# A graph network with experts on one Trainium2 core: other places for the experts' buffers, the second z weights loaded earlier, source rows made by TensorE, marks in bfloat16, and bounds and first attention weights within z

## The chip, the cores and the metric

The kernel runs on one core of one Trainium2 chip, in one launch. Its time is the device time in microseconds (us), the median over several runs. One of its executions is also recorded by the hardware profiler; all durations of single instructions come from that record. The engines are called as the profile calls them: PE is TensorE (matrix products and transposes), PEld its loading of weights, DVE is VectorE, ACT is ScalarE, POOL is GpSimd, SP is SyncE. SP and POOL also issue DMA transfers, each in the order of its own queue, and an engine's q (PEq, POOLq) is its sequencer, which runs branches and issues.

## The reference

There are 1250 nodes with 1024 features and 20000 edges `src -> dst`. Four parts follow each other, each on a layer norm of x and each added to x:

1. Graph attention with 4 heads of 256 columns. `z = norm(x) W`, `el = z . a_l`, `er = z . a_r` for each head; for every edge `e = leaky_relu(el[src] + er[dst], 0.2)`; over the edges into each node a softmax of e; the node's new value is the sum of `alpha * z[src]`.
2. A feed-forward part: small block matrices ("rails"), a GELU, and a large projection `h @ w_cproj.T` with 16384 inner columns.
3. A graph convolution: `h = norm(x) W + b`, and a sum of `h[col]` over edges and self loops, scaled by the square roots of the degrees.
4. A shared GEGLU expert, plus, for each row, the one of 8 experts with the largest logit: `gelu(x w1) * (x w2) @ w3`.

## The kernel before

All sizes are fixed: 1250 rows are 10 tiles (`T`) of 125 rows (`R`). Nearly everything is float32. The work is written in program order, and the framework orders each engine's instructions from it, with waits where buffers or data demand them; pools give buffers their places in SBUF, on the left or on the right side. A buffer in a place that something else held waits for the last use of what lay there.

**Counts and z(0), to 155 us.** For every tile the edges become counts of edges between nodes: one-hot rows `os` and `od` (kept in a pool with `HOT` buffers each) and PE products `pc` (L335). The counts go to DRAM (`cnt_d`), are turned into `CT` (int16: for each source tile all destinations), and `mark` (L296) writes `nm`, which is -1e30 where two nodes have no edge and 0 where they have one, to `nm_d`. In the same loop a tile of x (`xt`, `load_x`) is normalized and turned into `xT`, and `z_tile(0, t)` (L215) multiplies it with the weights of heads 0 and 1: 16 matmuls L218, a copy by ACT (L219) and four sums by DVE (L223), which give el and er. The weights come by `z_weights(g)` (L207): 8 transfers of 256 KB into `W` and two 250 KB broadcasts of a_l and a_r into `aw`, all issued by POOL. `W` has one buffer. `Z[0]` lies in `BZ`, a place that later stages use again, `Z[1]` in a buffer of its own.

**Branch L375.** Edges outside the expected windows are counted again under a condition, which does not hold for these inputs. Every engine runs the branch (L376).

**z(1), 165 to 236 us.** The same products for heads 2 and 3. Beside them DVE computes, for heads 0 and 1, the maxima over sources: `maxima(0)` (L394) adds a tile's marks `nm2` (loaded by SP from `nm_d`, 547 KB each) to `els`, the el of all sources in one row that all 125 partitions hold, and takes the maximum (L401): 20 of them. `els` comes by `el_rows` (L198): one transposition, a row written to DRAM, and a broadcast load, both issued by POOL. `degrees(t)` (L315) sums CT's rows, for the graph convolution's degrees. Then `bounds(0)` (L405) turns the maxima into two rows per head: for head 0 by 20 transposes of a column spread over all columns (L425), for head 1 through DRAM.

**Attention, 245 to 460 us.** `attend(h, b, between)` (L499) does one head and one half of the destinations: for each of ten source tiles DVE makes `u` (L504), ACT its exponential (L505), DVE the weights `w` (L508: times the count), and PE five products (L510) that add up in `po`; DVE then scales and adds to `X` (L520). Between the steps of the second and third call DVE runs `maxima(1)`, for heads 2 and 3, whose `els` is made by `el_rows(1)`. `X` is loaded by POOL (L448).

**Projection, to 2300 us.** The feed-forward part as a plan of fast matrix products in blocks (L675 in `product`), then the graph convolution (L1051 and around, to 2510 us), whose PE products read `xT`'s place last at about 2499 us.

**Shared expert and experts, 2510 us to the end.** `hidden` (L1118 and on; products `pab` at L1125) for the shared expert reads its weights `w12s` from `BZ`. The normalized rows lie in `xn_d` in DRAM, and POOL scatters the token list `tok`. For each expert, `weights12` and `weights3` load 2 MB and 1 MB (issued by SP, L987 to L992), an indirect transfer by POOL gathers up to 224 rows in two parts into `xg` (L1215), PE turns them (L1221), `hidden` and a product L1231 follow, and the result goes to `ys_d`. At the end the rows are gathered from there and added.

Of the kernel before, what the change touches and what calls it, by code (L numbers as in the profile page):

```python
# [30 lines left out]
GS, GD, HI, LO = 50, 25, 5, 250  # L31
HOT = 27
NEG = -1.0e30
# [69 lines left out]
def gnn_ffn_kernel(ctx, tc, x, src, dst, gat_w, a_l, a_r, maker, up, cproj,  # L103
# [15 lines left out]
    cnt_t = cnt_d.rearrange("g m l -> (g m l)").rearrange("(c p t j) -> t p c j", c=T, p=R, t=T)  # L119
    nm_d = dram.tile([GS, R, LO], F32, name="nm_d")  # L120
    nm_t = nm_d.rearrange("g m l -> (g m l)").rearrange("(t r n) -> t r n", t=T, r=R)
# [54 lines left out]
    Z = (BZ[:R].rearrange("p (t h f) -> p t h f", t=T, h=2), zp.tile([R, T, 2, F + 1], F32, name="Z"))  # L176
    for z in Z:
        nc.gpsimd.memset(z[:, :, :, F:F + 1], 1.0)
    deg = zp.tile([R, T, T], F32, name="deg")
    el, er, mx, el2, el8 = (zp.tile([R, H, T], F32, name=n) for n in ("el", "er", "mx", "el2", "el8"))  # L180
    xT = xTp.tile([P, KD, NP], F32, name="xT")
    elp = gat.enter_context(tc.tile_pool(name="elp", bufs=1, side="right"))

    def to_row(pool, psp, cols, k, n):
# [9 lines left out]
    def spread(dst_t, row):  # L194

        nc.gpsimd.dma_start(dst_t, row.rearrange("k r -> (k r)").partition_broadcast(R))

    def el_rows(g, pool, psp):  # L198
        els = elp.tile([R, 2, N], F32, name="els")
        spread(els.rearrange("p a n -> p (a n)"),  # L200
               to_row(pool, psp, el[:, 2 * g:2 * g + 2, :].rearrange("p h t -> p (h t)"), 2 * T, f"el{g}"))
        return els

    with tc.tile_pool(name="gw", bufs=1) as gwp, tc.tile_pool(name="gps", bufs=3, space=PSUM) as psp:
        W, aw = {}, {}

        def z_weights(g):  # L207
            W[g] = gwp.tile([P, KD, 2, F], F32, name="W")
            for k in range(KD):
                nc.gpsimd.dma_start(W[g][:, k], gat_w[2 * g:2 * g + 2, k * P:(k + 1) * P, :].rearrange("h p f -> p h f"))  # L210
            aw[g] = gwp.tile([R, 2, 2, F], F32, name="aw")
            for i, a in enumerate((a_l, a_r)):
                nc.gpsimd.dma_start(aw[g][:, i], a[2 * g:2 * g + 2, :].partition_broadcast(R))

# [11 lines left out]
        with tc.tile_pool(name="cc", bufs=1) as ccp, tc.tile_pool(name="cw", bufs=2) as cwp:  # L226
# [69 lines left out]
            def mark(d):  # L296
                nm = cwp.tile([R, HI, LO], F32, name="nm", bufs=1)
                nc.vector.tensor_scalar(nm, cns[d], 0.0, NEG, op0=ALU.is_equal, op1=ALU.mult)
                dma(nc.sync, nm_d[d * HI:d * HI + HI].rearrange("g m l -> m g l"), nm)

            def turn_counts(d):
                cn = cns[d]
                CTv = CT.rearrange("p (h a) n -> p a h n", a=2)
                for blocks in ([(g, 0) for g in range(4)], [(g, 1) for g in range(4)], [(4, 0), (4, 1)]):
# [7 lines left out]
                    else:  # L312
                        nc.scalar.copy(CTv[:, :, :, d0:d0 + GD], pt[:, :2].rearrange("p a (q h) -> p a h q", h=HI))

            def degrees(d):  # L315
                nc.vector.tensor_reduce(deg[:, d, :], CT[:, :, d * R:(d + 1) * R], AX.X, ALU.add)

            with tc.tile_pool(name="hot", bufs=1) as hotp, tc.tile_pool(name="gl", bufs=2) as lnp:
# [20 lines left out]
                def load_x(t):  # L339
                    xt[t] = lnp.tile([R, D], F32, name="xt", bufs=3)  # L340
                    dma(nc.sync, xt[t], x_t[t])

                for t in range(3):
                    load_x(t)
                z_weights(0)
                hots(0)
                count(0)
# [12 lines left out]
                for t in range(T):  # L360
# [9 lines left out]
                    if t + 3 < T:  # L370
                        load_x(t + 3)
                z_weights(1)
            els0 = el_rows(0, cwp, psp)

# [19 lines left out]
        def maxima(g, mxp, els):  # L394

            for d in range(T):
                nm = mxp.tile([R, N], F32, name="nm2", bufs=3 - g)
                dma(nc.sync, nm, nm_t[d])
                for h in (2 * g, 2 * g + 1):
                    sc = mxp.tile([R, N], F32, name="sc2")  # L400
                    nc.vector.tensor_tensor_reduce(sc, nm, els[:, h - 2 * g, :], scale=1.0, scalar=-3.0e38,  # L401
                                                   op0=ALU.add, op1=ALU.max, accum_out=mx[:, h, d:d + 1])
                    yield

        def bounds(g, pool, psp, rowp):  # L405
# [10 lines left out]
            for h in range(2):  # L416
                rows[2 * g + h] = rowp.tile([R, 2, N], F32, name="rr", bufs=2)
                if 2 * g + h == 0:

                    for i in range(2):  # L420
                        for t0 in range(0, T, 4):
                            n = min(4, T - t0)
                            pb = psp.tile([P, 4, R], F32, name="pt")
                            for t in range(n):
                                nc.tensor.transpose(pb[:R, t, :], bd[:, h, i, t0 + t:t0 + t + 1].to_broadcast([R, R]),  # L425
                                                    ident[:R, :R])
                            copy = nc.vector.tensor_copy if t0 == 4 else nc.scalar.copy
                            copy(rows[0][:, i, t0 * R:(t0 + n) * R], pb[:R, :n, :].rearrange("p a b -> p (a b)"))
                    continue
                spread(rows[2 * g + h].rearrange("p a n -> p (a n)"),  # L430
                       to_row(pool, psp, bd[:, h].rearrange("p a t -> p (a t)"), 2 * T, f"bd{2 * g + h}"))

        rows = {}
        rowst = ExitStack()
        rowp = rowst.enter_context(tc.tile_pool(name="rowp", bufs=1, side="right"))
        with tc.tile_pool(name="mx0", bufs=1) as mxp:
            search = maxima(0, mxp, els0)
            for t in range(T):
                for _ in range(3):
                    next(search, None)  # L440
                z_tile(1, t)
                degrees(t)
            bounds(0, mxp, psp, rowp)

# [50 lines left out]

    with tc.tile_pool(name="att", bufs=3) as atp, tc.tile_pool(name="aps", bufs=6, space=PSUM) as aps, \
            tc.tile_pool(name="tps0", bufs=2, space=PSUM) as tps:

        def attend(h, b, between=iter(())):  # L499
            po = [aps.tile([R, F + 1], F32, name="po") for _ in range(HT)]  # L500
            r1, r2 = (rows[h][:, i, b * HN:(b + 1) * HN] for i in range(2))
            for s in range(T):
                u = atp.tile([R, HN], F32, name="u")
                nc.vector.scalar_tensor_tensor(u, r1, el8[:, h, s:s + 1], r2, op0=ALU.add, op1=ALU.max)  # L504
                nc.scalar.activation(u, u, AF.Exp, bias=el2[:, h, s:s + 1])  # L505
                w = atp.tile([R, HN], F32, name="w")

                nc.vector.scalar_tensor_tensor(w, u, 2.0, CT[:, s, b * HN:(b + 1) * HN], op0=ALU.min, op1=ALU.mult)  # L508
                for i in range(HT):
# [13 lines left out]
        with tc.tile_pool(name="mx1", bufs=1) as mxp:  # L523
# [7 lines left out]

            nc.vector.tensor_reduce(dis, deg.rearrange("p d s -> p s d"), AX.X, ALU.add)
            nc.vector.tensor_scalar(dis, dis, 1.0, None, op0=ALU.add)
            nc.scalar.activation(dis, dis, AF.Sqrt)
# [576 lines left out]
    with back_end:  # L1111
# [3 lines left out]
        with tc.tile_pool(name="ab", bufs=2, space=PSUM) as abp, tc.tile_pool(name="tps", bufs=2, space=PSUM) as tps, \  # L1115
# [88 lines left out]

            with tc.tile_pool(name="w12", bufs=2) as w12p, tc.tile_pool(name="w3p", bufs=2) as w3p, \
                    tc.tile_pool(name="xg", bufs=3) as xgp, tc.tile_pool(name="xgT", bufs=2) as xgTp, \
                    tc.tile_pool(name="hp", bufs=2) as hp, tc.tile_pool(name="yp", bufs=3, side="right") as yp:
# [126 lines left out]
```

## Time and profile before

| | us |
|---|---|
| median of 3 runs | 2812.83 |
| lowest, highest | 2807.91, 2813.6 |
| the profiled execution, its own time | 2814.6 |
| its span (first to last record) | 2812.9 |
| PE busy | 2724.5 |
| DVE busy | 1604.8 |
| ACT busy | 887.3 |
| POOL busy | 781.1 |
| the 320 products of z (L218), 512 columns each | 141.5 |
| attention products of heads 0 and 1 (L510), first group of 400 | 96.7 |

The profile's page gives busy time by engine, the busy share in 40 slices of the span, the DMA queues, the chain of work that ended last, and the groups of instructions that cost most. Its trace answers closer questions: the list of waits (who waited for whom, for how long in total, how often, and the longest), the timeline of a stretch (start, length, engine, line, operation, `out<-in`, count, and in brackets the idle time before and what ended it), windows (busy time of each engine in a stretch, with the granted clock of TensorE, the share of the DMA engines in use, and GB/s), and all instructions of one line. Line numbers are those of the kernel before, unless a text says after.

### The profile page before, as it was taken

The numbers are of one execution on the slowest core, as the hardware profiler recorded it, in microseconds if no ns is written. First come the engines' busy times: TensorE is split into PE (matmuls) and PEld (weight loads), VectorE is DVE, ScalarE is ACT, GpSimd is POOL, SyncE is SP. The second block draws the span as 40 slices with busy tenths as digits, with TensorE's granted clock in tenths as the row PEclk, the third lists the DMA queues.
The fourth block names the chain that finished last, engine by engine and source line by source line (L and its number), as shares of the span: only waits on it lengthen the run. The fifth ranks groups of instructions, "written<-read, shape, count | busy, mean of one in ns | idle before, by whom it ended". The sixth has DMA issues, their size and how long they took to land. (4 is left out here: it accounts for less than half of the span.)

```text
span 2812.9 us, 31800 instructions
## 1 busy us (share of the span) xinstructions
PE 2724.5 (97%) x11009; PEld 1868.6 (66%) x11009; DVE 1604.8 (57%) x2704; ACT 887.3 (32%) x1545; POOL 781.1 (28%) x1118
## 2 busy tenths in 40 slices
PE   8989899999999999999999999999999999998997
PEld 5646677666766766667667667666666754765774
DVE  8766977755556566555556466555546764520124
ACT  2313235444343343343443443433432011210000
POOL 2011000234434434344344344343432110111001
PEclk9999999999999999999999999999999999999999
DMA  6464423579999999999999999999997540623665
GB/s 167 122 172 118 120 59 132 186 176 169 220 179 206 207 181 225 183 164 203 181 168 199 173 178 194 166 196 181 146 229 220 166 75 0 122 61 108 229 213 166
DMA packets 268759, 461.13 MB, mean 164 GB/s; under 512 B 49252, under 2 KB 145810, under 8 KB 267959
## 3 DMA queue, kind: packets, MB, share of 16 engines
q0 software_dynamic: 129296, 279.93, 57.7%
q1 hardware_dynamic: 139288, 179.00, 21.0%
q8 instruction: 94, 1.54, 0.2%
q14 instruction: 81, 0.66, 0.1%
HBM read 182.72 MB, written 276.09 MB: 163 GB/s over the span
## 5 line engine op out<-in xcount | busy, mean ns | idle before, releaser
L688 POOL DMA_DIRECT2D acc_d<-low x686 | 594.7, 867 | 906.4 <-ACT low L684 885.0
L684 ACT COPY low<-po 128x626 f32<-128x626 f32 x735 | 501.0, 682 | 951.1 <-PE po L675 895.2
L675 PE MATMUL po<-X,arena 128*128 128x313 f32 x2208 | 619.4, 427 | 0.5 <-DVE X L668 0.4
L675 PEld LDWEIGHTS po<-X,arena 128*128 128x128 f32 x2208 | 415.2, 189 | 176.2 <-ACT low L684 16.0
L675 PE MATMUL po<-low,arena 128*128 128x313 f32 x1520 | 429.4, 428 | 0.0
L675 PEld LDWEIGHTS po<-low,arena 128*128 128x128 f32 x1520 | 285.6, 189 | 121.1 <-ACT low L684 11.6
L675 PE MATMUL po<-X,first_w 128*128 128x313 f32 x776 | 222.1, 428 | 0.0
L675 PE MATMUL po<-X,BZ 128*128 128x313 f32 x720 | 206.8, 430 | 0.0
L675 PEld LDWEIGHTS po<-X,first_w 128*128 128x128 f32 x776 | 145.6, 189 | 62.7 <-ACT low L684 7.6
L675 PE MATMUL po<-low,first_w 128*128 128x313 f32 x624 | 178.7, 427 | 2.6 <-DVE low L668 1.6
L675 PEld LDWEIGHTS po<-X,BZ 128*128 128x128 f32 x720 | 136.2, 191 | 58.5 <-ACT low L684 5.8
L675 PEld LDWEIGHTS po<-low,first_w 128*128 128x128 f32 x624 | 117.4, 189 | 52.3 <-ACT low L684 4.4
L218 PE MATMUL pz<-W,xT 128*125 128x512 f32 x320 | 141.5, 600 | 7.8 <-PEq L376 7.8
L668 DVE TENSOR_TENSOR X<-X 128x626 f32<-128x626 f32 x125 | 101.0, 812 | 68.6 <-PE po L675 59.5
L675 PE MATMUL po<-low,BZ 128*128 128x313 f32 x480 | 137.8, 428 | 0.0
L668 DVE TENSOR_TENSOR arena<-arena 128x512 f32<-128x512 f32 x126 | 86.4, 688 | 63.9 <-PE po L675 63.3
L668 DVE TENSOR_TENSOR X<-X,low 128x626 f32<-128x626 f32 x105 | 84.7, 810 | 56.4 <-PE po L675 46.0
L675 PEld LDWEIGHTS po<-low,BZ 128*128 128x128 f32 x480 | 90.0, 189 | 38.5 <-ACT low L684 3.7
L510 PE MATMUL po<-BZ,w 125*125 125x257 f32 x400 | 96.7, 402 | 18.6 <-DVE w L508 17.4
L668 DVE TENSOR_TENSOR X<-low,X 128x626 f32<-128x626 f32 x101 | 82.6, 823 | 54.9 <-PE po L675 49.0
L218 PEld LDWEIGHTS pz<-W,xT 128*125 128x125 f32 x320 | 60.1, 191 | 80.7 <-issue 79.8
L660 ACT ACTIVATE X<-pz 128x626 f32<-128x626 f32 (+8 forms) x220 | 101.6, 524 | 17.9 <-PE pz L488 17.9
(308 smaller groups left out, 3384.8 us busy)
## 6 DMA issues: line engine op xcount, KB each, us to landing
acc_d<-low POOLq DMA_DIRECT2D x735, 313.0 KB, 6.2
arena<-in_cproj SPq DMA_DIRECT2D x148, 256.0 KB
w<-in_w SPq DMA_DIRECT2D x16, 1024.0 KB
BZ<-in_cproj SPq DMA_DIRECT2D x56, 256.0 KB
first_w<-in_cproj SPq DMA_DIRECT2D x52, 256.0 KB
nm<-nm_d SPq DMA_DIRECT2D x20, 546.9 KB
w3t<-in_w SPq DMA_DIRECT2D x8, 1024.0 KB
low<-acc_d SPq DMA_DIRECT2D x19, 313.0 KB
```

The source lines that it names most:

```text
L218: nc.tensor.matmul(pz, xT[:, k, t * R:(t + 1) * R], W[g][:, k], start=(k == 0), stop=(k == KD - 1))
L510: nc.tensor.matmul(po[i], w[:, i * R:(i + 1) * R], Z[h // 2][:, s, h % 2, :], start=(s == 0), stop=(s == T - 1))
L660: nc.scalar.activation(view(key)[:, :, n0 - n * NQ:n1 - n * NQ], pz[:, 2 * i:2 * i + 2, a + n0 - c0:a + n1 - c0], AF.Gelu)
L668: tt(view(k), *a, op=ALU.add if sign == "+" else ALU.subtract)
L675: nc.tensor.matmul(po[:, o, :NQ], view(x)[:, q, o * P:(o + 1) * P], view(y)[:, q, :], start=(i == q == 0), stop=(i + 1 == len(pairs) and q ...
L684: nc.scalar.copy(part, po[:, :, :NQ])
L688: sent[:] = [nc.gpsimd.dma_start(out=acc_d[p - 1, i - 1], in_=part, accum_op=ALU.add).ins]
```

## The change

- **Experts' places apart.** The pool of the experts' first weights (`w12`) moves to the right side, into xT's old place; the pool of gathered rows (`xg`) is opened first on the left, in a place that BZ does not cover.
- **Second z weights early.** `W` gets two buffers, and the second weights are asked for within the z(0) loop, at the third tile. The instructions as built show them on POOL right behind the first weights and the memsets of the limits, ahead of the zero fills of `tok_d` and `ys_d`.
- **Attention vectors on SP.** `aw` is loaded in a function of its own, `head_weights`, by SP and not by POOL.
- **Source row by PE.** For heads 0 and 1 `els` is made by `rows_by_array`: 20 transposes of a column spread over 125 columns, and six copies by ACT and DVE, in place of the way through DRAM. `bounds(0)` uses the same function for head 0, as before.
- **Marks in bfloat16.** `nm_d`, `nm` and `nm2` are bfloat16.
- **Places before the branch.** `nm` and `xt` lie in `Z[1]`, which nobody needs until z(1); the ones in `Z[1]`'s last column are set after the branch. `HOT` is 32 in place of 27.
- **Degrees on ACT.** Each tile's sum is a copy by ACT with an accumulated output; the last sum over tiles goes.
- **Bounds and first weights within z.** `bounds(0)` stands before the eighth tile of z(1), and the first three weights of attention before the tenth; the attention pool `att` is opened earlier for that, on the right.
- The instructions as built move two other things: the twenty maxima of heads 2 and 3 on DVE stand between the 21st and the 30th weights (before: between the 18th and the 31st), and the row of `els` for heads 2 and 3 stands on POOL behind the 20 loads of `X` (before: ahead of them).

```
-HOT = 27
+HOT = 32
...
-    nm_d = dram.tile([GS, R, LO], F32, name="nm_d")
+    nm_d = dram.tile([GS, R, LO], BF16, name="nm_d")
...
-    for z in Z:
-        nc.gpsimd.memset(z[:, :, :, F:F + 1], 1.0)
-    deg = zp.tile([R, T, T], F32, name="deg")
+    nc.gpsimd.memset(Z[0][:, :, :, F:F + 1], 1.0)
+    early = Z[1].rearrange("p t h f -> p (t h f)")
+    deg = zp.tile([R, T], F32, name="deg")
...
+    def rows_by_array(row, cols, psp):
+        for t0 in range(0, T, 4):
+            n = min(4, T - t0)
+            pb = psp.tile([P, 4, R], F32, name="pt")
+            for t in range(n):
+                nc.tensor.transpose(pb[:R, t, :], cols[:, t0 + t:t0 + t + 1].to_broadcast([R, R]), ident[:R, :R])
+            copy = nc.vector.tensor_copy if t0 == 4 else nc.scalar.copy
+            copy(row[:, t0 * R:(t0 + n) * R], pb[:R, :n, :].rearrange("p a b -> p (a b)"))
...
-            W[g] = gwp.tile([P, KD, 2, F], F32, name="W")
+            W[g] = gwp.tile([P, KD, 2, F], F32, name="W", bufs=2)
...
+        def head_weights(g):
             aw[g] = gwp.tile([R, 2, 2, F], F32, name="aw")
             for i, a in enumerate((a_l, a_r)):
-                nc.gpsimd.dma_start(aw[g][:, i], a[2 * g:2 * g + 2, :].partition_broadcast(R))
+                nc.sync.dma_start(aw[g][:, i], a[2 * g:2 * g + 2, :].partition_broadcast(R))
...
-                nm = cwp.tile([R, HI, LO], F32, name="nm", bufs=1)
+                nm = early[:, :HN].bitcast(BF16).rearrange("p (g l) -> p g l", l=LO)
...
-            def degrees(d):
-                nc.vector.tensor_reduce(deg[:, d, :], CT[:, :, d * R:(d + 1) * R], AX.X, ALU.add)
...
-                    xt[t] = lnp.tile([R, D], F32, name="xt", bufs=3)
+                    xt[t] = early[:, N + t % 3 * D:][:, :D]
...
-                z_weights(1)
-            els0 = el_rows(0, cwp, psp)
+                    if t == 2:
+                        with tc.issue_after(made[-1].ins):
+                            z_weights(1)
+            elp = gat.enter_context(tc.tile_pool(name="elp", bufs=1, side="right"))
+            head_weights(1)
+            els0 = elp.tile([R, 2, N], F32, name="els")
+            for h in range(2):
+                rows_by_array(els0[:, h, :], el[:, h, :], psp)
...
-                nm = mxp.tile([R, N], F32, name="nm2", bufs=3 - g)
+                nm = mxp.tile([R, N], BF16, name="nm2", bufs=3 - g)
...
+        nc.gpsimd.memset(Z[1][:, :, :, F:F + 1], 1.0)
...
+        atp = rowst.enter_context(tc.tile_pool(name="att", bufs=3, side="right"))
+
+        def weight(h, b, s):
+            r1, r2 = (rows[h][:, i, b * HN:(b + 1) * HN] for i in range(2))
+            u = atp.tile([R, HN], F32, name="u")
+            nc.vector.scalar_tensor_tensor(u, r1, el8[:, h, s:s + 1], r2, op0=ALU.add, op1=ALU.max)
+            nc.scalar.activation(u, u, AF.Exp, bias=el2[:, h, s:s + 1])
+            w = atp.tile([R, HN], F32, name="w")
+            nc.vector.scalar_tensor_tensor(w, u, 2.0, CT[:, s, b * HN:(b + 1) * HN], op0=ALU.min, op1=ALU.mult)
+            return w
...
             for t in range(T):
                 for _ in range(3):
                     next(search, None)
+                if t == 7:
+                    bounds(0, mxp, psp, rowp)
+                if t == T - 1:
+                    first_weights = [weight(0, 0, s) for s in range(3)]
                 z_tile(1, t)
-                degrees(t)
-            bounds(0, mxp, psp, rowp)
+                nc.scalar.activation(mxp.tile([R, N], I16, name="copy"), CT[:, t, :], AF.Copy, accum_out=deg[:, t:t + 1])
...
+                w = first_weights.pop(0) if first_weights else weight(h, b, s)
...
-            nc.vector.tensor_reduce(dis, deg.rearrange("p d s -> p s d"), AX.X, ALU.add)
-            nc.vector.tensor_scalar(dis, dis, 1.0, None, op0=ALU.add)
+            nc.vector.tensor_scalar(dis, deg, 1.0, None, op0=ALU.add)
...
-            with tc.tile_pool(name="w12", bufs=2) as w12p, tc.tile_pool(name="w3p", bufs=2) as w3p, \
-                    tc.tile_pool(name="xg", bufs=3) as xgp, tc.tile_pool(name="xgT", bufs=2) as xgTp, \
+            with tc.tile_pool(name="w12", bufs=2, side="right") as w12p, tc.tile_pool(name="xg", bufs=3) as xgp, \
+                    tc.tile_pool(name="w3p", bufs=2) as w3p, tc.tile_pool(name="xgT", bufs=2) as xgTp, \
```

More of the change, by code (lines that the diff above doesn't have):

```diff
@@ L176, in gnn_ffn_kernel @@
     Z = (BZ[:R].rearrange("p (t h f) -> p t h f", t=T, h=2), zp.tile([R, T, 2, F + 1], F32, name="Z"))
-    for z in Z:
-        nc.gpsimd.memset(z[:, :, :, F:F + 1], 1.0)
-    deg = zp.tile([R, T, T], F32, name="deg")
+    nc.gpsimd.memset(Z[0][:, :, :, F:F + 1], 1.0)
+    early = Z[1].rearrange("p t h f -> p (t h f)")
+    deg = zp.tile([R, T], F32, name="deg")
     el, er, mx, el2, el8 = (zp.tile([R, H, T], F32, name=n) for n in ("el", "er", "mx", "el2", "el8"))
     xT = xTp.tile([P, KD, NP], F32, name="xT")
-    elp = gat.enter_context(tc.tile_pool(name="elp", bufs=1, side="right"))
     def to_row(pool, psp, cols, k, n):
@@ L345, in gnn_ffn_kernel @@
                 z_weights(0)
+                head_weights(0)
                 hots(0)
@@ L420, in bounds @@
                     for i in range(2):
[L421 to L428, printed above, removed]
+                        rows_by_array(rows[0][:, i, :], bd[:, h, i, :], psp)
                     continue
@@ L494, in gnn_ffn_kernel @@
     YS = [XX.rearrange("p t d -> p (t d)")[:, i * 2 * NQ:(i + 1) * 2 * NQ].rearrange("p (q n) -> p q n", q=2) for i in range(16)]
-    with tc.tile_pool(name="att", bufs=3) as atp, tc.tile_pool(name="aps", bufs=6, space=PSUM) as aps, \
-            tc.tile_pool(name="tps0", bufs=2, space=PSUM) as tps:
+    with tc.tile_pool(name="aps", bufs=6, space=PSUM) as aps, tc.tile_pool(name="tps0", bufs=2, space=PSUM) as tps:
         def attend(h, b, between=iter(())):
             po = [aps.tile([R, F + 1], F32, name="po") for _ in range(HT)]
-            r1, r2 = (rows[h][:, i, b * HN:(b + 1) * HN] for i in range(2))
             for s in range(T):
[L503 to L508, printed above, removed]
+                w = first_weights.pop(0) if first_weights else weight(h, b, s)
                 for i in range(HT):
```

## The prediction

> **What bounds the kernel now.** I read the page's busy tenths in 40 slices first, then the chain of waits, the list of waits of the first 500 us, and the timeline around each gap that these named.
>
> ```profile
> PE   8989899999999999999999999999999999998997
> ```
>
> TensorE (PE) is busy 2724.5 of 2812.9 us. From slice 7 to slice 35 (a slice is 70.3 us) nothing else can be late for long, so a change pays only where PE stands still or is slow: slices 2 to 6 and 36 to 39. The chain that ended last shows the second of these places:
>
> ```profile
> 2521.76 56.08 PE pab L1125 x160
> ...
> 2578.63 9.13 DMA xg<-xn_d,tok
> ...
> 2587.90 3.52 PE pt L1221 x16
> 2591.41 14.44 PE pab L1125 x64
> ...
> 2616.16 12.26 PE pab L1125 x64
> ```
>
> After the last product of the shared expert (2577.84) PE waits until 2587.90 for the first gathered rows. Then it runs slowly: the same 64 products take 14.44 us for the first expert and 12.26 for the second.
>
> The waits and the timeline show the first place, between the two halves of z:
>
> ```profile
> POOL W L210 <- PE pz L218: 132.2, 1, 132.2
> PE pz L218 <- PEq L376: 7.8, 1, 7.8
> ```
>
> ```profile
> 149.20 0.51 SPq L111 DMA_DIRECT2D nm_d<-nm  x1
> 153.83 0.33 SPq L110 DMA_DIRECT2D nm<-nm_d  x1
> 155.55 5.77 POOL L210 DMA_DIRECT2D W<-in_gat_w  x8 [132.22 <-PE pz L218]
> 164.79 8.26 DVE L316 TENSOR_REDUCE deg<-CT 125x10 f32<-125x1250 int16 x6 [7.05 <-DVEq L376]
> 165.24 35.08 PE L218 MATMUL pz<-W,xT 128*125 128x512 f32 x77 [7.79 <-PEq L376]
> ```
>
> GpSimd (POOL) can load the second weights only when z(0) has left the buffer (155.25), and at the branch L376 PE stands 7.8 us. And after z:
>
> ```profile
> 165.24 70.70 PE L218 MATMUL pz<-W,xT 128*125 128x512 f32 x160 [7.79 <-PEq L376]
> 235.78 2.45 PE L425 MATMUL pt<-ident,bd 125*125 125x125 f32 x18
> ...
> 244.89 26.50 PE L510 MATMUL po<-BZ,w 125*125 125x257 f32 x106 [4.89 <-DVE w L508]
> ```
>
> PE turns the bounds, then waits 4.89 us for the first attention weights. The windows give the granted clock (PEclk, the last column but two) in both places and in the stretch where VectorE (DVE) is full:
>
> ```profile
> 236.00:245.00 9.00, 3.14 (x23) 2.33 (x21) 6.12 (x17) 6.25 (x11) 3.93 (x10) 0.75 0.23 56
> 245.00:285.00 40.00, 38.97 (x165) 32.65 (x166) 31.95 (x43) 15.25 (x24) 8.90 (x17) 0.93 0.74 179
> 285.00:340.00 55.00, 42.27 (x169) 32.32 (x168) 55.00 (x90) 12.90 (x26) 1.55 (x3) 0.94 0.39 107
> 2578.00:2596.00 18.00, 8.10 (x29) 7.07 (x30) 1.78 (x3) 1.06 (x2) 4.78 (x5) 0.62 0.97 306
> ```
>
> **Experts' places apart.** Before, the buffer of the first gather lies over BZ, which holds the shared expert's weights, and the expert weights wait for the same last product. After, the weights lie on the right, in xT's old place (last read at about 2499), and the gather in a place that nobody holds: it waits only for the stores of xn_d and for the token list, ready at about 2543. POOL has been idle for 36.4 us at 2578.63, so it can issue then; the gather took 9.13 us, so it lands near 2553 and leaves 25 us over. The two experts' weights now stand on SyncE's (SP's) queue ahead of the shared w3 and of the last tile's store of xn_d. 3 to 6 MB at the 306 GB/s of the last window are 10 to 20 us; from 2499 they end by 2519, and even if the store came last of all the gather would land in time. So the 10.06 us go. PE no longer idles, so its clock should stay full: the 16 transposes cost about 2.8 us (3.52 at mostly half clock; 8 at full clock took 1.04, and two evictions lie between) and the 64 products 12.2. From 2577.84 to the end of the products: 28.0 us before, 15.0 after. **−13.0 us** (bounds −12.0 and −13.5). All of it is on the path, since PE is the bound from there to 2766.
>
> The row on the clock: the window 2578:2596 stands at 0.62, that is 13.7 us at one half. The half clock thus outlasted the restart at 2587.9 by some 7.8 us. [...]
>
> **Second weights early, rows by TensorE: the start of z(1).** With two buffers the 2 MB go out right behind the first weights (POOL, about 16 to 23 us), past the zero fills, which are not needed for two milliseconds. PE is the bound from 24 us; the first z product at 24.85 could come later by 1 us or not at all: 0 (±1). At 155 us what remains before the branch is 20 small transposes (18 took 2.45 us) between copies on ScalarE (ACT) and DVE. Most need el of earlier tiles, so PE reaches the branch at about 158.1, as before (157.8). The branch is where the cost lies:
>
> ```profile
> L376 PEldq COMPARE_BRANCH  x1: 7134/7134/7134, 157.8 to 157.8; - x1
> ```
>
> The other branch, L1071, took PE 3754 ns at 2404.3. At L376 the weights' 2 MB filled the transfer engines at that moment (share 0.99 in 155 to 165 us); they are gone after. I take 3.75 us: z(1) starts at 162.2 in place of 165.24, **−3.0 us**. If the branch is slow for its own sake it stays at 165.3 (0). In their place only two 250 KB loads of the attention vectors, now on SP, lie in that window.
>
> **The end of z(1).** Before, from the start of z(1) to the first attention product: 244.89 − 165.24 = 79.65 us, and the first products run at half clock (0.93 over the window 245:285 is 5.6 us at one half), some 2.8 us lost: 82.5 in all. After: z 70.5; the bounds' 21 transposes within it 3.3 (2.45 + 0.48 + 0.27, and a short wait); the weights are there when z ends; the one transposition of head 2's and 3's el still waits for the last sums, 1.4 us, and stands early among the attention products. 75.2 in all: **−7.3 us** (bounds −5 and −9).
>
> This needs DVE to be ready. Its first maximum was at 184.59, held by the broadcast source row; with the row made in place it is at about 166. 20 maxima at 1.38 us and five tiles' sums at 1.4 end at about 202.8 (27.6 and 7 us, and the small steps of the bounds); the bounds are wanted at the eighth tile, 162.2 + 50 = 212.2. Slack 9.4 us. The ten degree sums leave DVE (8.26 + 5.54 us) for ACT, which is busy 5.53 of 71 us there; ten passes at about 1.4 us (0.56 for 500 columns of CT) hide.
>
> **Marks in bfloat16.** The marks' loads halve (546.9 to 273 KB) and their stores go in runs of 500 bytes instead of 1000. The stores' row: the last is issued by 149.71, and the loads that wait for it at 153.83, while the first maximum comes at 166: 12 us hide it, twice over. 0. [...]
>
> Is the maximum itself slower with a 16-bit operand? The nearest rows are two like operations on 625 columns: w with the int16 CT took 0.81 us, u with float operands only 0.87. I take no change, either way. HOT 32, xt's and the marks' new place: PE is the bound there, 0 (±1).
>
> **New cost in attention.** DVE is full from 284 to 332 us: the 20 maxima of heads 2 and 3 stand among its weights from the 18th to the 31st. After, they stand between the 21st and the 30th, so four steps fewer hide them. A step is 2.17 us of PE and 1.63 of DVE (starts of w: 254.66 and 256.83 where PE paces, 274.75 and 276.38 where DVE does), so 4 × 0.54: **+2.2 us** (0 to 4). Their source row is now issued on POOL behind all 20 loads of X; it lands some 35 to 41 us into attention, its first user is at 42. Cover up to 7 us; if that is gone, each us late costs one.
>
> **Sum.** −13.0 − 3.0 − 7.3 + 2.2 = **−21.1 us**. The profiled execution (2814.6, with 1.7 around its span) becomes 2793.5. It lies 1.8 above the median of the runs, so the median of 2812.83 becomes **2791.7**.
>
> **Rivals.**
>
> A, the middle gives little: the branch stays at 7.1 us (+3.0), the source row of heads 2 and 3 comes late (up to +5), or the transposes inside z cost more. For it: the branch was seen slow at this place, and the order on POOL. Against it: the full transfer engines explain it. −11 to −18, 2795 to 2802.
>
> B, the tail's gap is filled by another wait: the token list or the last store late. For it: 6 MB now go ahead. Against it: 25 us over, in a stretch where the transfer engines' share is 0.04. Then −8, about 2805; with both A and B it is within 0.2% (5.6 us, about what a measurement of this kernel can tell from no change).
>
> C, slower: the maximum pays x us for its bfloat16 operand. Twenty stand in the full stretch, 20x on the path, and twenty within z, where 9.4 us are free: 20x + (20x − 9.4). Against the 21.1 it decides from x = 0.76 us, an operation of 2.14 instead of 1.38. At x = 1 it is +9.5, 2822. For it only that the form is not in this trace; against it the 0.81 beside 0.87.
>
> D, deeper: no half clock at the start of z(1), and the new attention cost hides: −25 to −27, 2786 to 2788.
>
> **How the numbers follow.** Forecast (−18 to −25) 0.60; A 0.23; B alone 0.05; D 0.04; A and B together, no change that can be told, 0.03; C 0.05. Faster: 0.60 + 0.23 + 0.05 + 0.04 = 0.92. The range, 2787 to 2801, holds the forecast and most of A, some 0.80; it leaves out A's end, most of D, B, C and no change.
>
> **What would show it.** In the profile after: the first gather issued before 2560 (old time) and no PE gap behind the shared expert, clock 1.00 there, 64 products in 12.2 us. COMPARE_BRANCH L376's counterpart at 3 to 5 us and the z products from about 162. First maximum at about 166, pitch 1.38; the bounds' transposes inside z without a gap; attention from about 237. DVE full from about 285 − 10 and PE's waits in it some 2 us more. I am wrong if the maximum's pitch rises, if PE waits on a source row in attention, or if the tail shows a new wait for the token list.

## The result

| | before | after |
|---|---|---|
| median, us | 2809.3 (5 runs) | 2792.36 (5 runs, 2787.66 to 2794.37) |
| ratio of the runs | | 0.9934, 95% interval 0.992 to 0.9949 |
| span of the profiled execution, us | 2812.9 | 2790.0 |

The change makes the kernel faster by 0.66%, 18.5 us of 2809 (14 to 22); the two medians in the table lie 16.9 us apart. In a second comparison on one chip (run `again` below) the ratio was 0.9925 (0.9903 to 0.9946). The forecast was 21.1 us less. The two profiled spans lie 22.9 us apart, and that difference can be followed step by step.

The busy row of the page after:

```profile
PE   8999899999999999999999999999999999999998
```

The 7 in the last slice but one is gone, and slice 2 has risen from 8 to 9. The timeline of PE after, from z(1) to the end of attention's first half:

```profile
163.95 50.38 PE L227 MATMUL pz<-W,xT 128*125 128x512 f32 x112 [5.26 <-PEq L389]
214.16 2.45 PE L201 MATMUL pt<-ident,bd 125*125 125x125 f32 x18
...
217.63 19.91 PE L227 MATMUL pz<-W,xT 128*125 128x512 f32 x46
238.22 1.56 PE L524 MATMUL po<-BZ,w 125*125 125x257 f32 x6 [0.68 <-ACT Z L228]
239.62 0.27 PE L185 MATMUL pt<-ident,el 125*20 125x125 f32 x1
...
262.85 21.04 PE L524 MATMUL po<-BZ,w 125*125 125x257 f32 x96 [0.92 <-DVE X L534]
...
348.17 1.84 PE L524 MATMUL po<-Z,w 125*125 125x257 f32 x6
351.39 0.84 PE L504 MATMUL pt<-BZ 128*128 128x128 f32 x4 [1.38 <-POOL BZ L498]
```

The wait at the branch is 5.26 us where it was 7.79. The bounds' transposes stand inside z with no idle time before them, and attention begins 0.68 us after z, where 4.89 us of waiting for w and the transposes had stood between. The windows of the same trace show that the clock does not fall there any more (third column from the right: 1.00 and 1.00 where it was 0.75 and 0.93):

```profile
236.00:245.00 9.00, 8.32 (x36) 6.19 (x35) 5.00 (x14) 1.94 (x4) 4.88 (x12) 1.00 0.40 108
245.00:285.00 40.00, 38.49 (x175) 32.11 (x173) 33.03 (x45) 14.58 (x27) 6.76 (x13) 1.00 0.57 139
```

The timeline of PE after around the shared expert and the first expert:

```profile
2499.13 13.16 PE L1138 MATMUL pab<-low,BZ 128*128 128x417 f32 x32 [0.33 <-DVE lg L1115]
...
2512.70 56.21 PE L1138 MATMUL pab<-low,BZ 128*128 128x417 f32 x160
2568.75 1.04 PE L1234 MATMUL pt<-ident,xg 128*128 128x128 f32 x8
2570.26 0.88 PE L1234 MATMUL pt<-ident,xg 96*128 96x96 f32 x8 [0.48 <-DVE xgT L1237]
2571.46 12.37 PE L1138 MATMUL pab<-xgT,w 128*128 128x224 f32 x64 [0.32 <-DVE xgT L1237]
```

The first expert's transposes follow the shared products at once, and its 64 products take 12.37 us. The first line is a surprise: the same 32 products took 11.47 us before.

The same points of PE in both traces, as stretches:

| stretch | before | after | difference |
|---|---|---|---|
| start to the start of z(1) | 165.24 | 163.95 | −1.3 |
| to attention's first product | 79.65 | 74.27 | −5.4 |
| to the first product of heads 2 and 3 | 110.48 | 109.95 | −0.5 |
| over the rails' first products to the next call of attention | 32.15 | 28.72 | −3.4 |
| to the shared expert (projection, convolution) | 2122.22 | 2122.24 | 0.0 |
| to the end of the first expert's products | 95.95 | 84.54 | −11.4 |
| to the end | 207.21 | 206.33 | −0.9 |

The sum is −22.9. The last but one holds two things: 27.9 us between the last shared product and the end of the first expert's became 14.8 (−13.1), and the 32 products took 1.7 more. The last stretch took between 206.3 and 208.1 us in all 14 profiles, so its −0.9 is within what comes and goes.

### The profile page after: what moved, and what is told of

Same layout as the page of the kernel before. It is cut to its first block, busy times and chain, and to the rows that moved or that the text cites. A ratio compares the mean times of both kernels' runs of the same rounds, so it can differ in the third digit from the quotient of the medians.

```text
span 2790.0 us, 31868 instructions
## 1 busy us (share of the span) xinstructions
PE 2722.3 (98%) x11028; PEld 1865.6 (67%) x11028; DVE 1594.1 (57%) x2695; ACT 900.6 (32%) x1568; POOL 780.4 (28%) x1112
```

## The experiments

Stretches are taken from one profile of each run. Most repeat to about 0.3 us where nothing is changed. Some jump when TensorE's granted clock falls to one half within them (0.50 from 245 to 250 us in the kernel before), often by the same amount: the 32 shared products took 11.47 or 13.16 us, the stretch over the rails 27.04 or 28.72 in two profiles of the changed kernel itself, 96 attention products 21.04 or 22.73, each time about 1.7 us apart. So a difference of 1.7 us or less in one profile needs a look at the clock before it gets a cause. Whole times repeat less well: from the call of attention after the rails to the shared expert, where no edit touches anything, the profiles took between 2116.4 and 2130.9 us. The longer ones show PE waiting in single spots of the projection. So verdicts on parts come from stretches, and whole times are given for what they are.

**The tail alone.** The kernel before with only the last two lines of the diff (`w12` on the right, `xg` ahead of `w3p`).

> The kernel before with the experts' places apart and nothing else. Theory: the tail's gain does not need the rest. The first expert's transposes follow the shared expert at once, the stretch from the last product of the shared expert to the end of the first expert's products falls from 28.0 us to about 15, and the time falls by 12 to 14 us (ratio 0.9953). z and attention stay as before: z(1) starts at about 165.2, the first products of heads 2 and 3 at about 355.4. Rival 1: the new load traffic on SP at 2499 slows the shared expert's first products every time (they took 11.47 us before and 13.16 after): then 13.2 here too, and the gain is 11 to 12. Rival 2: that half clock is chance, and the same 32 products take 11.5 here.

Measured: ratio 0.9965 (0.9949 to 0.998), about −10 us (6 to 14). PE's timeline of this run:

```profile
2516.68 56.21 PE L1125 MATMUL pab<-low,BZ 128*128 128x417 f32 x160
2572.72 1.04 PE L1221 MATMUL pt<-ident,xg 128*128 128x128 f32 x8
...
2575.44 12.37 PE L1125 MATMUL pab<-xgT,w 128*128 128x224 f32 x64 [0.32 <-DVE xgT L1224]
```

The stretch is 14.8 us, as in the changed kernel, and z(1) starts at 165.56 as before: this part needs nothing of the rest. The first 32 products took 11.47 us here with the same loads going on, so the loads are not what slows them.

**Everything but the tail.** The changed kernel with those two lines undone.

> The changed kernel with the experts' places as before. Theory: what is left is the gain up to attention, 7 us at the first products of heads 2 and 3 (348 against 355.4), and whatever the rails after attention give (3.4 us more in the profile of the changed kernel). The tail's 28 us from the last shared product to the end of the first expert's products come back. Time: 8 to 11 us below the kernel before (ratio about 0.9966). Rival: the 3.4 us at the rails were chance; then 7 us (0.9975) and the rails' wait for POOL is near 3.8 us again.

Measured: 0.9961 (0.9947 to 0.9974), about −11 us. Its chain of waits has the tail of before again:

```profile
2567.13 8.49 DMA xg<-xn_d,tok
...
2575.75 3.52 PE pt L1234 x16
2579.27 13.25 PE pab L1138 x64
```

From the end of the shared expert to the end of the first expert's products it takes 26.0 us, so the two halves add up (0.9965 times 0.9961 is 0.9926). The rails' stretch is 28.72 us, as after. It took 27.0 to 29.6 us in the 12 profiles with the middle part and 30.1 (`tail_only`) and 32.15 (before) in the two without it. So the gain goes with the middle part, but its size is not fixed: it is 0.5 to 5 us by these profiles.

**What makes the branch slow.** Two runs change only what is transferred beside it. The first loads the first weights once more after z(0) and never uses them (`z_weights` takes its index modulo the four heads for that):

```
+                z_weights(2)
...
             head_weights(1)
```

> The changed kernel with 2 MB more to load: after z(0) the first weights are loaded once more into their old place and never used. This puts the traffic of the kernel before back beside the branch, without anything that waits for it. Theory: the branch waits for instructions that come by the same transfer engines; PE's branch takes about 7.1 us as before and not 4.8, z(1) starts at about 166.3 and the time is 2 to 3 us above the changed kernel. Rival: the branch is slow for another reason (its distance, or the engines that it waits for); then it stays at 4.8 us and z(1) at 164.

The second moves the attention vectors away from it (`aw` has two buffers for that, and the scrap `sc` of the sums one in place of two):

```
                             z_weights(1)
+                        head_weights(1)
...
-            head_weights(1)
```

> The changed kernel with the second attention vectors loaded right behind the second weights in place of just before the branch (two buffers for them, one for the sums' scrap). Theory: no transfers stand beside the branch, so PE's branch takes 3.7 us, as the later one that runs beside idle transfer engines (3754 and 3652 ns), z(1) starts 1 us earlier (about 162.9), and DVE's branch ends earlier than 166.3. The time falls by about 1 us. Rival: the 500 KB are not what makes the branch slow; it stays at 4.8 us.

And one run loads the second weights late again, in one buffer, with all the rest of the change in place:

```
-            W[g] = gwp.tile([P, KD, 2, F], F32, name="W", bufs=2)
+            W[g] = gwp.tile([P, KD, 2, F], F32, name="W")
...
-                    if t == 2:
-                        with tc.issue_after(made[-1].ins):
-                            z_weights(1)
+                z_weights(1)
```

> The changed kernel with one buffer for the z weights, so that the second weights are loaded after z(0), as before. All else stays. Theory: this part is worth what stands at the branch. PE's branch takes about 7 us again, z(1) starts 1.5 to 2.5 us later (counted from the first transpose of el: 10 to 11 us in place of 8.5), and the time is about 2 us longer. Rival: the weights themselves land after the branch; then z(1) starts 3 us later or more and PE waits for W.

All instructions of the branch's line, PE's branch alone, from the changed kernel, `aw_early`, `loaded_branch` and `w_late` in this order (count, shortest/median/longest in ns, start):

```profile
L389 PEldq COMPARE_BRANCH  x1: 4832/4832/4832, 158.8 to 158.8; - x1
```

```profile
L389 PEldq COMPARE_BRANCH  x1: 3552/3552/3552, 159.9 to 159.9; - x1
```

```profile
L390 PEldq COMPARE_BRANCH  x1: 5729/5729/5729, 159.7 to 159.7; - x1
```

```profile
L387 PEldq COMPARE_BRANCH  x1: 6292/6292/6292, 158.6 to 158.6; - x1
```

With no transfers beside it PE's branch takes 3.6 us, with 0.5 MB of attention vectors 4.8, with 2 MB more 5.7 and 6.3, and 7.1 in the kernel before. The mean share of the DMA engines in use from 159 to 163 us goes the same way: 0.03 in `aw_early`, 0.34 in the changed kernel, 0.79 in `loaded_branch`, 0.83 in `w_late`, 1.04 before. So the transfers lengthen the branch; what the branch waits for, instructions that come by the same engines or something else, no run shows. The theory holds in its order and not in its size: `loaded_branch` was expected at 7.1 and gave 5.7, and `w_late`, which has the second weights where they were before, was expected at about 7 and gave 6.3. From the start of the last group of z(0) products to z(1) it is 16.2 us before, 14.5 after, 13.3 in `aw_early`, 15.5 in `loaded_branch`, 16.1 in `w_late`. So the early weights are worth 1.5 us at this place, and 2.9 with the vectors early too (`aw_early`). The whole times, as ratios to the kernel before, are 0.9907 (0.9884 to 0.9929) for `aw_early`, 0.9937 (0.9915 to 0.9959) for `loaded_branch` and 0.9933 (0.9908 to 0.9958) for `w_late`, and tell none of them from the changed kernel; the 3.5 us by which `aw_early`'s profile is ahead at the shared expert come from the projection (2118.7 us).

The compare-and-branch at this place took 45 to 76 ns on DVE, ACT, SP and POOL; PE's took 3.4 us (`both`) to 7.3 us (`tail_only`), and in `row_dram` PE stood 5.75 us before z(1).

**Bounds after z again**, without weights ahead.

```
-                if t == 7:
-                    bounds(0, mxp, psp, rowp)
-                if t == T - 1:
-                    first_weights = [weight(0, 0, s) for s in range(3)]
...
+            bounds(0, mxp, psp, rowp)
+            first_weights = []
```

> The changed kernel with the bounds after z(1), as before, and no weights made ahead; everything else of the change stays. Theory: PE turns the bounds after z, waits some 4 to 5 us for u, the exponential and w, and starts attention at half clock: the end of the first call (first products of the second call, 262.9 in the changed kernel) comes 5 to 7 us later. The loss in the full stretch of VectorE stays (2 us), since the maxima of heads 2 and 3 still stand between the 20th and the 30th weights. Rival: the early source row alone made the bounds early enough, and moving them into z saves no more than the transposes' time beside z; then 0 to 2 us.

Measured, in PE's timeline:

```profile
163.84 71.21 PE L227 MATMUL pz<-W,xT 128*125 128x512 f32 x160 [5.32 <-PEq L389]
234.89 2.45 PE L201 MATMUL pt<-ident,bd 125*125 125x125 f32 x18
...
241.69 26.23 PE L522 MATMUL po<-BZ,w 125*125 125x257 f32 x106 [2.75 <-DVE w L451]
268.83 21.47 PE L522 MATMUL po<-BZ,w 125*125 125x257 f32 x98 [0.92 <-DVE X L532]
```

The second call starts 6.0 us later than in the changed kernel (262.85), with z(1) started at the same time. From the start of z(1) to the products of heads 2 and 3 it takes 189.9 us against 184.2. Between these two points the kernel before took 190.1 us. So the bounds within z and the three weights made ahead, which this run takes out together, are nearly all that the change gains here; the wait for w is 2.75 and not 4.89 us (before, u had itself waited 2.29 us for a store of another head's row, and does not here). The ratio was 0.9948 (0.9929 to 0.9967).

**Degrees on VectorE again**, as ten sums.

```
-                nc.scalar.activation(mxp.tile([R, N], I16, name="copy"), CT[:, t, :], AF.Copy, accum_out=deg[:, t:t + 1])
+                degrees(t)
```

> The changed kernel with the degrees as ten sums on VectorE again (1.45 us each, between the maxima). Theory: in the changed kernel the bounds were ready at 208.0 and wanted at 214.2, 6 us of cover. 14.5 us more on VectorE make them ready at 222, so PE stands about 8 us at the bounds' transposes within z, and the time is 6 to 9 us longer than the changed kernel's. Rival: the order puts the sums where VectorE is idle (it stood 11.7 us for the first marks), and nothing changes.

DVE reached the bounds at 218.00 us instead of 207.26, but PE's timeline shows only this:

```profile
165.13 53.72 PE L227 MATMUL pz<-W,xT 128*125 128x512 f32 x118 [5.29 <-PEq L392]
219.97 2.70 PE L201 MATMUL pt<-ident,bd 125*125 125x125 f32 x20 [1.13 <-issue]
```

The expectation was wrong by a factor of three to four. Three of the ten sums found the time in which DVE waited for the first marks, and the framework put the transposes six products later (118 ahead of them, not 112). z with the bounds takes 2.2 us more, where 6 to 9 were expected: PE stands 1.13 us at the transposes, and some 0.8 us are half clock at the start of z(1) (granted clock 0.50 from 168 to 170 us, 0.97 in the changed kernel). Ratio 0.9944 (0.9922 to 0.9965).

**The first source row through DRAM again.**

```
-            els0 = elp.tile([R, 2, N], F32, name="els")
-            for h in range(2):
-                rows_by_array(els0[:, h, :], el[:, h, :], psp)
+            els0 = el_rows(0, cwp, psp)
```

> The changed kernel with the first source row through DRAM, as before (store, then broadcast load, both on POOL). Theory: the row was late before because it stood behind 2.5 MB of weights on POOL's queue and on the transfer engines. With the weights early the store goes out at about 158 and the row lands at 170 to 176, beside the marks, which land at 170.9 in any case. The first maximum comes 0 to 5 us later, the bounds at 208 to 213, still ahead of 214, so the time stays within 1 us: this part of the change is worth nothing beside the early weights. Rival: the branch on POOL and SP holds the row as it held the marks, the first maximum comes after 180, and PE waits 3 to 10 us at the bounds.

DVE's timeline of this run, its first maximum and the start of the bounds, which stand at 170.87 and 207.26 in the changed kernel:

```profile
177.47 1.46 DVE L412 CUSTOM_DVE_ANT_0 sc<-nm,els 125x1250 f32<-125x1250 bf16 x1 [18.99 <-DMA nm<-nm_d]
...
214.62 0.17 DVE L422 TENSOR_TENSOR top<-mx,er 125x20 f32<-125x20 f32 x1
```

The first maximum comes 6.6 us later, a little more than expected. The bracket names the marks' load, but the row's own load fits as well: it was issued at 165.19 and took 11.8 us to land. The cover of the bounds is used up, and yet PE's timeline shows hardly a wait there:

```profile
164.13 51.23 PE L227 MATMUL pz<-W,xT 128*125 128x512 f32 x112 [5.75 <-PEq L387]
```

Attention's first product comes 1.0 us later, counted from the start of z(1). Of this, 0.85 us is that the same 112 products ahead of the bounds take 51.23 us in place of 50.38: the granted clock is 0.50 from 168 to 170 us, where the changed kernel has 0.97. The bounds' transposes follow these products at once. No run shows that the late row slows the clock. Up to heads 2 and 3 another 0.9 us is lost; there DVE's order has moved a little (the first maximum of heads 2 and 3 at 281.14 where 279.96 was). PE's 20 transposes ahead of the branch, which this run saves, give 0.4 back. So with the weights early the row by TensorE is worth 1.5 us in this profile, of which 0.85 is clock; the whole time (0.993, 0.9906 to 0.9954) does not tell it.

**Where the maxima of heads 2 and 3 stand.** Two runs test the loss in attention. One asks for the loads of X after the second source row:

```
-    for t in range(T):
-        dma(nc.gpsimd, X[:, t, :], x_t[t])
...
             els1 = el_rows(1, mxp, tps)
+            for t in range(T):
+                dma(nc.gpsimd, X[:, t, :], x_t[t])
```

> The changed kernel with the loads of X asked for after the source row of heads 2 and 3 and not before it. The row's store then starts at about 240 in place of 257, and the maxima stand on VectorE from the 8th weights on in place of the 21st. Theory: they would lie beside PE's work and the full stretch shrinks, but the row comes by DRAM (6 us to store, 11 to load) and lands at about 257 while the first maximum is reached at 250: VectorE stands some 7 us, of which the weights ahead cover 4. Then the gain of the longer spread (up to 6 us) and this wait nearly cancel: -4 to +2 us against the changed kernel. Rival: where the maxima stand does not matter, since VectorE is full for its whole work in any case; then only the wait shows, +3 to +7.

The other makes that row like the first, by TensorE:

```
-            els1 = el_rows(1, mxp, tps)
+            els1 = elp.tile([R, 2, N], F32, name="els")
+            for h in range(2):
+                rows_by_array(els1[:, h, :], el[:, 2 + h, :], tps)
```

> The changed kernel with the source row of heads 2 and 3 made as the first one: 20 transposes and six copies. The maxima then stand from the 4th to the 30th weights. Theory: the full stretch is too little time for the maxima, not too much work. VectorE has 24 u, 27 w, 20 maxima, 15 sums into X and copies from 240 on, about 80 us, so it ends at about 320 with the 30th weights, PE pays 2.7 us for the transposes and saves the waits: the first products of heads 2 and 3 come 3 to 6 us earlier than 348.2, and the time is 3 to 6 us below the changed kernel's (ratio to the kernel before about 0.9915). Rival: the transposes and the copies cost what the spread saves; then within 1 us.

`row_first` lies in the expected range: DVE waits 2.1 us for the row, until 255.43, where 7 had been expected, and the stretch from attention's start to heads 2 and 3 still falls from 109.95 to 106.90 us (ratio 0.9922, 0.9901 to 0.9944). `row_array` does better than expected: 101.04 us, with 1.3 us of transposes ahead of the first product besides. Its windows and the end of its full stretch:

```profile
245.00:285.00 40.00, 37.01 (x163) 31.12 (x162) 38.11 (x57) 12.69 (x20) 6.55 (x13) 0.96 0.59 151
285.00:320.00 35.00, 30.34 (x132) 23.46 (x130) 35.00 (x60) 11.07 (x23) 0.53 (x1) 1.00 0.11 29
```

```profile
320.51 21.04 PE L524 MATMUL po<-BZ,w 125*125 125x257 f32 x96 [0.63 <-DVE X L534]
341.38 1.84 PE L524 MATMUL po<-Z,w 125*125 125x257 f32 x6
```

DVE (third busy column) is busy 38.11 of 40 us in the first window, where the changed kernel has 33.03. The work is the same; its first maximum stands 38 us earlier than the changed kernel's at 279.96, and the maxima lie beside PE's products:

```profile
241.70 1.46 DVE L414 CUSTOM_DVE_ANT_0 sc<-nm,els 125x1250 f32<-125x1250 bf16 x1
```

Two different edits that bring the row earlier both shorten the stretch. That settles the cause: the loss is in where the maxima stand, and that follows from when their row arrives. From the start of z(1) to heads 2 and 3 the run takes 176.6 us against 184.2 (−7.6). Its ratio to the kernel before is 0.989 (0.9874 to 0.9906). The changed kernel's were 0.9934 (0.992 to 0.9949) and 0.9925 (0.9903 to 0.9946): below both, though the last interval just touches its own.

**Both improvements together.** `row_array` and `aw_early` in one kernel.

> The changed kernel with the source row of heads 2 and 3 by TensorE (as in row_array) and the second attention vectors early (as in aw_early). Theory: the two add up. PE's branch takes 3.6 us and not 4.8, so z(1) starts 8.5 - 7.2 = 1.3 us earlier, counted from the first transpose of el, and the stretch from the start of z(1) to the first products of heads 2 and 3 is 176 to 177 us as in row_array. Time about 1 us below row_array, 11 to 13 below the changed kernel; ratio to the kernel before about 0.9885. Rival: the earlier start is given back at the full stretch of VectorE, because the maxima of z(1) set its pace; then the same as row_array.

Measured: 0.9902 (0.988 to 0.9924), the same as `row_array` alone. The branch took 3.4 us and z(1) began 13.0 us after the last z(0) group, 1.6 earlier, as expected; but attention to heads 2 and 3 takes 104.73 us in place of 101.04, and the gain is given back. 1.7 of this is half clock: one group of 96 products took 22.73 us in place of 21.04. The other 2 us lie in this group:

```profile
292.51 16.58 PE L524 MATMUL po<-BZ,w 125*125 125x257 f32 x66 [2.32 <-DVE w L451]
```

At the pace at which `row_array`'s group there runs (54 products in 11.94 us), 66 take 14.6. The granted clock is 0.57 from 293 to 297 us, where `row_array` has 1.00. But DVE is busy nearly all the time beside it, and its maxima stand a step later (behind the 4th weights, not the 3rd), so which of the two sets the 2 us stays open.

**The changed kernel again**, beside the three last kernels on one chip.

> The changed kernel once more, beside the others on one chip. Theory: 17 to 21 us below the kernel before (ratio 0.9925 to 0.994), branch 4.8 to 5.2 us, attention's first product 74.3 us after the start of z(1), the first products of heads 2 and 3 184.2 us after it, from the end of the shared expert to the end of the first expert's products 14.9 us. The first 32 products of the shared expert take 11.5 or 13.2 us, as the half clock falls or not. Rival: the first profile was a lucky one at the rails after attention; then their wait for POOL is above 2 us here.

Measured: 0.9925 (0.9903 to 0.9946), 2788.93 against 2811.16 us. Branch 4.77 us; attention's first product 74.59 us and heads 2 and 3 184.55 us after the start of z(1); 14.76 us to the end of the first expert's products; rails' wait 1.38 us. These lie within 0.4 us of the first profile. The first 32 products took 11.47 us, and the rails' stretch 27.04 us in place of 28.72: both are 1.7 us of clock.

## Why the prediction was right, and where its steps were not

**The tail, −13.0: measured −13.1.** POOL issued the gather well ahead:

```profile
2535.07 1.01 POOL L1228 DMA_INDIRECT xg<-xn_d,tok  x1 [1.48 <-DMA tok<-tok_d]
```

That is 33.7 us before PE first uses the rows; they took 5.0 us to land, so nearly 29 us were over where 25 were reckoned. No new wait took the gap, and nothing was given back later. The size holds against the profile of before. Against `no_tail`, the same code at this place, it is 11.3 us (26.0 to 14.8): there the 64 products after the wait took 13.25 us, in the kernel before 14.44, without the wait 12.37. So after such a wait the products took 0.9 us longer in one profile and 2.1 us in the other than without one, and the tail's gain is 11.3 or 13.1 us by these profiles.

**The start of z(1), −3.0: measured −1.3 to −1.6.** This is the term that was mis-sized. The step that failed is "I take 3.75 us". The two loads of attention vectors were named just behind it and counted as nothing; with them the branch took 4.83 us, and without them 3.55. PE also reached the branch at 158.8 and not at 158.1, half of that because z(0) ran 0.3 us later. The mechanism, transfers beside the branch, was right.

**The end of z(1), −7.3: measured −8.2.** Before 82.5 us (79.65 and 2.8 lost at half clock), after 74.27. The 1.4 us for the last transposition were not paid: it found room between two attention products (0.11 us), and a wait of 0.68 us for the last copy of Z, which the prediction did not have, stands in its place. The reading of DVE was off: the first maximum came at 170.87 and not at 166, because the marks' loads left later than before the change. They stand on SP behind the branch, and the first leaves right after DVE's last step of the branch, not ahead of PE's branch as before (153.83):

```profile
L389 DVEq EVENT_SEMAPHORE  x1: 21/21/21, 166.3 to 166.3; - x1
```

```profile
166.75 0.32 SPq L110 DMA_DIRECT2D nm<-nm_d  x1
```

```profile
170.87 1.46 DVE L414 CUSTOM_DVE_ANT_0 sc<-nm,els 125x1250 f32<-125x1250 bf16 x1 [11.73 <-DMA nm<-nm_d]
```

In `aw_early` the same two points are 163.7 and 163.93. The cover was 6.2 us (bounds ready at 207.97, wanted at 214.16), not 9.4, and was enough. In `loaded_branch` and `w_late` the first maximum came at 176.43 and 174.94 without a loss in z; in `row_dram`, at 177.47, the cover was gone.

**Attention, +2.2: measured +2.3** (109.95 against 110.48 − 2.8). The reckoning by four steps fewer of 0.54 us gave the right size, and `row_first` and `row_array` show its cause. The late row was no wait of its own here: it was issued at 263.36, and the first maximum ran at 279.96 without waiting.

**Not in the sum.** The prediction has no term for the rails. Their first products came 2.4 us sooner and took 1.0 us less at half clock (0.50 from 362 to 366 us before, 0.57 from 352 to 356 after): −3.4 us (−5.1 in `again`, where 1.7 us less of half clock fell there). PE waited for POOL, and POOL before waited for a small load on SP's queue behind the first projection weights; the lines of POOL before and after:

```profile
359.57 0.40 POOL L475 TENSOR_TENSOR BZ<-BZ 128x128 f32<-128x128 f32 x1 [2.80 <-DMA BZ<-in_maker]
```

```profile
349.66 1.32 POOL L496 TENSOR_TENSOR BZ<-BZ 128x128 f32<-128x128 f32 x2
```

From the first product of heads 2 and 3 to the rails' first it took 3.2 to 4.5 us in the runs that keep the middle part, 5.6 and 4.8 in the two without it. Why that load lands sooner (it was issued 2.2 us before the end of the attention call in both) was not tried and stays open.

**By chance.** The 32 first shared products took 13.16 us in 3 of the 12 profiles with the places apart, and 11.47 in the rest. The granted clock was 0.57 from 2499 to 2502 us in the changed kernel's trace and 1.00 in the same place before. Just ahead of them PE has small products with gaps in both (busy 3.98 of 5 us after, 3.19 of 4 before, at clock 1.00). The changed kernel gave both values, 11.47 in `again`; what sets which, no run shows. Without this 1.7 us the profiled span would have been 24.6 us shorter.

**How near the total came.** The terms of the sum, −21.1, measured −20.3 together (−13.1, −1.3, −8.2, +2.3); the rails, the clock at the shared products and the last stretch, none of them in the sum, add −3.4, +1.7 and −0.9. That 2791.7 lies only 0.7 us from the median is partly luck. The forecast subtracts from a median of three runs, 2812.83, where five runs gave 2809.3. From there the medians fell by 16.9 us, which is in the range of A; by the ratio of the runs it is 18.5, just within the forecast's, and 21 in `again`.

**The rivals.** A held in one point: the branch stayed above the value taken, 4.8 us, not 7.1. B did not occur. C is out: the maxima took 1.46 us with bfloat16 marks, as with float32. D's first condition did not occur; that the full stretch can be hidden was shown by another edit. The forecast's own range, 2787.8 to 2794.8 from its base of 2812.83, held the median.

**Marks in bfloat16, HOT, the degrees.** The maximum's duration did not change (median 1.45 us before, 1.46 after). The stores of 500-byte runs cost nothing that the traces show: no wait for the marks' stores appears, and the marks' loads began at 166.75, right behind DVE's part of the branch. ACT hides the degrees' 14 us (166.6 to 180.6), but on VectorE they would have cost no more than 2.2 us (`deg_dve`). HOT was not tried alone; the z(0) groups lie within 0.5 us of before.

## What to carry to other kernels

When an engine has more to do than time in one stretch, ask first whether the same work could have started earlier: here the maxima waited for a row that took the way through DRAM behind twenty other loads, and making the row by 20 small transposes on TensorE, which cost 1.3 us, shortened the way from the start of z(1) to heads 2 and 3 by 7.6 us, where the whole change had gained 5.9. A buffer's place is a wait: two pools laid over a region that is read until the last moment held back 3 MB of loads and a gather, and moving them gave 13 us for two lines. A transfer that stands beside a branch is not free: 0.5 MB lengthened this one by 1.3 us. And half clock came and went between two profiles of one kernel by 1.7 us, as much as such a term, so compare the clock before a small difference is given a cause.

## What was not expected of the hardware

- PE's compare-and-branch took 3.4 to 7.3 us while the other engines' took 45 to 76 ns, and its length followed the transfers beside it: 3.4 and 3.6 us with none (`both`, `aw_early`), 4.8 to 5.2 with 0.5 MB, 5.7 and 6.3 with 2 MB more (`loaded_branch`, `w_late`), 7.1 and 7.3 in the two kernels that issue the second weights and their vectors there by POOL (before, `tail_only`). DVE's last step of the branch comes late too: at 166.3 us after, at 163.7 in `aw_early`, though its compare takes 76 ns.
- The projection, 2.1 ms of nearly unbroken products, took from 2116.4 to 2130.9 us in 14 profiles of kernels that do not differ there; its few waits come and go from run to run (PE was busy 18.44 of the 20 us from 860 on before, all 20 after) and are the noise of this measurement.
